# Offset convolutions two blocks ahead of the sampling, between an image's own steps

## The chip, the cores and the metric

The kernel runs on one core of a Trainium2 chip. The metric is the device time of one execution in microseconds, as the median of several runs. A profile was taken of one further execution.

## The reference

Four images of 256 channels and 64 by 64 pixels pass through two layers. This document is about the first, a deformable convolution with 3 by 3 taps:

```
x = groupnorm(x)                                    # 32 groups
om = conv3x3(x, w_off) + b_off                      # 27 channels
y, x positions = grid + tap + om[:18]               # per pixel and tap
mask = sigmoid(om[18:])
sampled = bilinear(x, positions) * mask             # four corners
out = einsum(sampled, w_conv)                       # 9 taps x 256 channels -> 256
```

Its sum with the input goes to the second layer: attention whose logits run over the images, and a mixture of eight experts of which each token takes two. Everything is float32.

## The kernel before

**Stages.** First comes the deformable convolution, image by image, then two passes of attention with routing, then the experts' tiles, then the weighing and the storing of the result. The change lies in the first stage alone.

**A sampling step.** A tile is 128 pixels, an image has 32 tiles (`NR`), each with 9 taps (`K2`), so an image has 288 steps (`STEPS`) and the whole stage 1152. For each image a table lies in memory (`tables[b]`), with two pixels, one above the other, in each row, so that one gathered run of 4 KB for each partition holds all four corners. A step n does the following:

- `gather` (L626, POOL): an indirect DMA from the table by the indices `params[b][0]` into one of ten buffers (`NGB`), two gathers every second step, ten steps ahead. The first of a pair waits for the last corner of step n + 1.
- `corner0` (L643, ScalarE) and `corner` (L651, VectorE, three a step) weigh the four corners with `params[b][1]` and add them into s.
- `turned` (L665, TensorE) transposes s, `to_sbuf` (L671, ScalarE) copies it out of PSUM, and `product` (L690, TensorE) multiplies it with the tap's weights into the tile's accumulator.
- `done` (L699 and L701) copies a finished tile out; after four tiles SP stores them.

On VectorE, ScalarE, TensorE and POOL the order of this loop is the order of the program (`manual_schedule`); SP's order is left to the planner.

**What an image needs first.** `pieces(b)` lists the preparation as pairs of a step and a function. `stats` (bn_stats, L332) at steps 32 to 47 and the group means after them give the scale and shift of the group norm; n is then 56. After that come eight blocks of 512 pixels (`NBLK`, `BLK`). `block(q, at)` can do two things:

- The table (`table`): `norm` (L393 or L395) normalises the block's rows into xs, `turn` and `leave` (L402, L415) transpose them, and four DMAs (L421) write them to the table.
- The offsets (`offsets`): TensorE multiplies ten rows of xs with the offset weights (`rows_of`, L433, 12 matmul instructions), ScalarE copies the result shifted for each of three taps (`shifted`, L445), TensorE adds these (`summed`, L454), and `kept` (L463) copies the 27 values of each pixel to SBUF.

`positions` (L492) then turns the offsets into indices and corner weights: 16 or 17 small operations on VectorE and one Sigmoid on ScalarE (L503).

**When.** Image 0's tables are made ahead of the first step, and so are the offsets of its first two blocks (`EARLY`). Its other six blocks' offsets lie between its own steps, at `(q - 2) * 36 + 12`, each followed by `positions` for that block's four tiles. Images 1 to 3 are prepared wholly during the image before: one block with table and offsets every 22 steps (`PERIOD`) from step 56, the offsets kept in a buffer for the whole image (`om`), and one call of `positions` for all 32 tiles at steps 235 to 251. So image 0's steps carry eight whole blocks of image 1 and six offset blocks of its own; those of images 1 and 2 carry eight whole blocks; those of image 3 carry none.

**Buffers.** The two images' raw data (`axs`), xs, the small tiles of `positions` (`atmp`) and the parameters are SBUF pools that stand one after another. The next stage's tiles reuse the same memory.

Of the kernel before, what the change touches and what calls it, by code (L numbers as in the profile page):

```python
# [9 lines left out]
F32 = mybir.dt.float32  # L10
# [7 lines left out]
P = 128  # L18
B, C, H, W = 4, 256, 64, 64
HW = H * W  # L20
NCH = C // P
K2 = 9
NR = HW // P
NOFF = 3 * K2
# [12 lines left out]
NT = BLK // P  # L37
# [3 lines left out]
STEPS = NR * K2  # L41
NGB = 10
AHEAD = NGB + 1
LOAD_AHEAD = 6
FIRST = 32
EARLY = 2
PERIOD = 22
NBLK = HW // BLK
GROUP = 8
# [29 lines left out]
def conv_attn_moe_kernel(  # L79
# [22 lines left out]
    nc = tc.nc  # L102
# [44 lines left out]
    def routed(rows, to, rw, ps_turned, ps_out, pool, name):  # L147


        pr, wTs = [], {}  # L150

        def turned(n):
            tp = ps_turned.tile([P, C], F32, name=f"{name}_tp{n}", tag="tp")
            for ch in range(NCH):
                T.transpose(tp[:, ch * P : (ch + 1) * P], rows[n][:, ch * P : (ch + 1) * P], ident)
            wTs[n] = pool.tile([P, C], F32, name=f"{name}_wT{n}", tag="sT")
            (V.tensor_copy if n % 2 else S.copy)(wTs[n], tp)

        def product(n):
            if not n:  # L160
                pr.append(ps_out.tile([P, len(rows), NX], F32, name=f"{name}_pr", tag="om"))
            for ch in range(NCH):
                T.matmul(
                    pr[0][:, n, :], wTs[n][:, ch * P : (ch + 1) * P], rw[:, ch, :],
                    start=(ch == 0), stop=(ch == NCH - 1),
                )

        for n in range(len(rows) + 1):
            if n < len(rows):
                turned(n)  # L170
            if n:
                product(n - 1)
            yield
        V.tensor_copy(to, pr[0].rearrange("p (ch k) n -> p ch k n", ch=NCH))
        yield
# [49 lines left out]
    with ExitStack() as actx:  # L225
        aw = actx.enter_context(tc.tile_pool(name="a_w", bufs=1))
        ag = actx.enter_context(tc.tile_pool(name="a_gather", bufs=1))
        asm = actx.enter_context(tc.tile_pool(name="a_sm", bufs=5))
# [4 lines left out]
        apad = actx.enter_context(tc.tile_pool(name="a_pad", bufs=2))  # L233
        atmp = actx.enter_context(tc.tile_pool(name="a_tmp", bufs=1))
        axs = [
            actx.enter_context(tc.tile_pool(name=f"a_x{i}", bufs=1)) for i in range(2)
        ]
        ps_tp = actx.enter_context(tc.tile_pool(name="ps_tp", bufs=4, space=PSUM))
        ps_om = actx.enter_context(tc.tile_pool(name="ps_om", bufs=2, space=PSUM))
# [77 lines left out]
        def pieces(b):  # L317
# [46 lines left out]

            xrv = xr.rearrange("p ch (h w) -> p ch h w", w=W)
            tv = tables[b].rearrange("(y x) (two c) -> y x two c", x=TW, two=2)
            om = atmp.tile([P, NR, NOFF], F32, name=f"om{b}", tag="om") if b else None

            def block(q, at, table=True, offsets=True, alone=False):

# [86 lines left out]
                        )  # L457

                def kept():
                    of[q] = om[:, rows_in(q), :] if b else atmp.tile(  # L460
                        [P, NT, NOFF], F32, name=f"om{b}_{q}", tag="om_", bufs=2
                    )
                    V.tensor_copy(of[q], t["pt"])  # L463

                out_.append((at, lambda: norm(0)))
# [21 lines left out]
            def rows_in(q):  # L487
                return slice(q * NT, (q + 1) * NT)
# [3 lines left out]
            def positions(rows, given, at, each):  # L492
                name = f"{b}_{rows.start}"
                nr = rows.stop - rows.start
                shape = [P, 2, nr, K2]
                t = {}

                def tmp(key, tag, dtype=F32, shape=shape):
                    t[key] = atmp.tile(shape, dtype, name=f"{key}{name}", tag=tag)
                    return t[key]  # L500

                def masked():
                    S.activation(  # L503
                        tmp("mask", "mask", shape=[P, nr, K2]), given()[:, :, 2 * K2 :],
                        AF.Sigmoid,
                    )

                def placed():
                    V.tensor_tensor(
                        tmp("pos", "pos"),  # L510
                        given()[:, :, : 2 * K2].rearrange("p r (k two) -> p two r k", two=2),
                        grid[:, :, rows], ALU.add,
                    )

                def indexed():
                    p0 = t["p0"]
                    V.tensor_scalar(
                        p0[:, 0], p0[:, 0], float(TW), float(TW + 1), ALU.mult, ALU.add
                    )
# [12 lines left out]

                def add(a, c):
                    V.tensor_tensor(a, a, c, ALU.add)

                def clamp():
                    V.tensor_scalar(t["pos"], t["pos"], -1.0, float(H), ALU.max, ALU.min)

                def compare():
                    V.tensor_tensor(tmp("over", "over"), t["p0"], t["pos"], ALU.is_gt)  # L540

                def rest():
                    V.tensor_tensor(tmp("lo", "over"), t["pos"], t["p0"], ALU.subtract)

                def other():
                    V.tensor_scalar(tmp("hi", "pos"), t["lo"], -1.0, 1.0, ALU.mult, ALU.add)

                done_ = []
                for i, fn in enumerate((
                    placed,  # L550
                    lambda: add(t["pos"], taps[:, :, rows]),
                    clamp,
                    lambda: V.tensor_copy(tmp("pi", "ki32", I32), t["pos"]),
                    lambda: V.tensor_copy(tmp("p0", "p0"), t["pi"]),
                    compare,
                    lambda: V.tensor_tensor(t["p0"], t["p0"], t["over"], ALU.subtract),
                    rest,
                    other,
                    indexed,
                    lambda: both("hi"),  # L560
                    lambda: both("lo"),
                    *(lambda c=c: weighted(c) for c in range(4)),
                )):
                    done_.append((at + i // each, fn))
                done_.append((at + 1, masked))
                return done_

            def place_for():
                params[b] = (
                    ap_.tile([P, NR, K2], I32, name=f"idx{b}", tag="idx"),  # L570
                    ap_.tile([P, 4, NR, K2], F32, name=f"wts{b}", tag="wts"),
                )

            if b:
                for q in range(NBLK):
                    block(q, n + q * PERIOD)
                n += (NBLK - 1) * PERIOD + 25
                later.append((n - 1, place_for))
                later.extend(positions(slice(0, NR), lambda: om, n, 1))
                assert n + 16 <= STEPS - AHEAD, n  # L580
                return later

            place_for()
            for q in range(NBLK):
                first.extend(block(q, n + 10 * q, offsets=False, alone=True))
            n += 10 * NBLK + 8
            for q in range(EARLY):
                at = n + 20 * q  # L590
                first.extend(block(q, at, table=False, alone=True))
                first.extend(positions(rows_in(q), lambda q=q: of[q], at + 25, 4))
            router = routed(
                [wconv_sb[:, ch, k, :] for ch in range(NCH) for k in range(K2)],
                wconv_sb[:, :, :, C:], rwc_sb, ps_tp, ps_om, asm, "wconv",
            )
            for m in range(NCH * K2 + 2):
                first.append((n + 10 + 1.5 * m, lambda: next(router)))
            for q in range(EARLY, NBLK):
                at = (q - 2) * NT * K2 + 12  # L600
                block(q, at, table=False)
                later.extend(positions(rows_in(q), lambda q=q: of[q], at + 25, 2))
                assert at + 33 <= q * NT * K2 - AHEAD, q
            order = {nc.vector.engine, nc.scalar.engine, nc.tensor.engine}
            with tc.manual_schedule(engines=order):
                emit(first)
            return later

        def emit(todo):
            for _, fn in sorted(todo, key=lambda p: p[0]):  # L610
                fn()
# [1181 lines left out]
```

## Time and profile before

| | us |
|---|---|
| median of 3 runs | 3588.42 (3581.35 to 3590.16) |
| the profiled execution | 3621.63 |
| its span, first to last instruction | 3619.9 |
| first sampling step of image 0, 1, 2, 3 | 73.1, 599.0, 1103.0, 1604.1 |
| last sampling step | 2121.7 |

Over the span TensorE's matmuls are busy 84%, VectorE 69%, POOL 54% and ScalarE 51%. An engine's busy share is a mean over stages with different limits, so the sampling steps are read by themselves. L643 runs exactly once a step; its start times, read from that line's instructions in the trace, give the pace of any stretch of steps.

### The profile page before, as it was taken

How to read it: one execution, taken by the hardware profiler on the slowest of the kernel's cores; microseconds unless marked ns; L12 is line 12 of the kernel's file. 1: busy time of each engine (PE TensorE's matmuls, PEld its weight loads, DVE VectorE, ACT ScalarE, POOL GpSimd, SP SyncE). 2: the span in 40 equal slices, each digit the busy share in tenths (PEclk: the TensorE clock that was granted, in tenths of full speed). 3: DMA queues.
4: the chain of work that ended last, by engine and by line, in shares of the span. 5: the costliest groups of instructions: out<-in, count | busy, mean ns of one | idle time of the engine just before them, and what ended most of it. 6: DMA issues, size and time to landing. Idle time of an engine off the chain costs nothing.

```text
span 3619.9 us, 49496 instructions
## 1 busy us (share of the span) xinstructions
PE 3041.8 (84%) x13658; PEld 2230.4 (62%) x13658; DVE 2480.5 (69%) x6303; ACT 1832.4 (51%) x4281; POOL 1961.6 (54%) x1818
## 2 busy tenths in 40 slices
PE   5899997899987899977777889997676588899996
PEld 4667665667665676656566655543343367788884
DVE  5867686777776777866666758875445555455887
ACT  2556554456554565544444457744344254455663
POOL 2555565666576665677666643305445536655441
PEclk8999998999998999989888989998788789999996
DMA  9889889899989899988787878723234334444888
GB/s 301 306 304 336 316 326 351 278 353 366 348 313 350 307 346 341 352 297 310 280 312 285 320 205 141 139 74 121 99 105 154 111 97 132 154 138 153 289 280 285
DMA packets 349897, 911.66 MB, mean 252 GB/s; under 512 B 43540, under 2 KB 123035, under 8 KB 347576
## 3 DMA queue, kind: packets, MB, share of 16 engines
q0 software_dynamic: 208704, 689.10, 55.1%
q1 hardware_dynamic: 140920, 219.39, 19.0%
q8 instruction: 113, 1.85, 0.2%
q14 instruction: 160, 1.31, 0.1%
HBM read 741.87 MB, written 170.12 MB: 252 GB/s over the span
## 4 chain that ended last, share of the span: by engine, by line
PE 48%; issue 14%; POOL 11%; DMA 9%; DVE 8%; another core or an unknown queue 6%; ACT 3%; SPq 0%; POOLq 0%; DVEq 0%; ACTq 0%
PE acc L690 13%; POOL g L626 10%; DMA g<-table,idx 6%; PE ph L1577 6%; PE py L1595 5%; PE tps L665 3%; PE po L433 3%; PE po L1129 3%; DVE s L651 3%; PE p_wq_sb L796 3%; PE p_wk_sb L796 3%; PE pg L796 2%; PE pv L796 1%; DVE mix L1098 1%
## 5 line engine op out<-in xcount | busy, mean ns | idle before, releaser
L651 DVE SCALAR_TENSOR_TENSOR s<-g,wts,s 128x256 f32<-128x256 f32 x3456 | 1433.5, 479 | 542.3 <-ACT s L643 374.3
L626 POOL DMA_INDIRECT g<-table,idx x1152 | 1310.4, 1137 | 765.7 <-DVE s L651 465.2
L690 PE MATMUL acc<-wconv_sb,sT 128*128 128x265 f32 x4608 | 1338.9, 415 | 274.3 <-ACT sT L671 165.7
L690 PEld LDWEIGHTS acc<-wconv_sb,sT 128*128 128x128 f32 x4608 | 832.4, 201 | 423.5 <-ACT sT L671 196.2
L671 ACT COPY sT<-tps 128x256 f32<-128x256 f32 x1152 | 425.4, 369 | 781.0 <-PE tps L665 489.9
L643 ACT ACTIVATE s<-g,wts 128x256 f32<-128x256 f32 x1152 | 588.9, 511 | 210.2 <-DMA g<-table,idx 180.9
L665 PE MATMUL tps<-ident,s 128*128 128x128 f32 x2304 | 461.7, 283 | 39.8 <-DVE s L651 37.8
L665 PEld LDWEIGHTS tps<-ident,s 128*128 128x128 f32 x2304 | 327.7, 148 | 270.1 <-issue 162.4
L1606 POOL DMA_INDIRECT ys_rows<-y,to x284 | 282.9, 996 | 299.9 <-DVE y L1603 225.2
L1577 PE MATMUL ph<-xT,w 128*128 128x256 f32 x1136 | 282.8, 392 | 35.6 <-DVE second L1563 18.3
L1273 POOL DMA_INDIRECT xs_rows<-u,slots x256 | 250.0, 976 | 94.6 <-issue 88.8
L1595 PE MATMUL py<-w,hT 128*128 128x256 f32 x1136 | 270.7, 381 | 0.0
L1581 ACT ACTIVATE hT<-ph,w 128x256 f32<-128x256 f32 x284 | 132.7, 474 | 237.2 <-PE ph L1577 170.0
L1577 PEld LDWEIGHTS ph<-xT,w 128*128 128x128 f32 x1136 | 210.3, 196 | 66.6 <-ACT hT L1581 18.4
L1600 DVE TENSOR_TENSOR y<-py,w 128x512 f32<-128x512 f32 x142 | 98.2, 691 | 206.8 <-ACT w L1539 70.7
L1595 PEld LDWEIGHTS py<-w,hT 128*128 128x128 f32 x1136 | 218.3, 192 | 30.5
L1098 DVE SCALAR_TENSOR_TENSOR mix<-pv,att,mix 128x512 f32<-128x512 f32 x192 | 131.0, 742 | 142.6 <-remote 106.3
L1103 ACT ACTIVATE gate<-pg,bg_c 128x512 f32<-128x512 f32 x64 | 43.8, 688 | 277.1 <-DVE mix L1118 190.1
L919 DVE SCALAR_TENSOR_TENSOR junk<-q,k 128x512 f32<-128x512 f32 x256 | 162.1, 687 | 24.6 <-ACT k L900 24.4
L433 PE MATMUL po<-xs,woff_sb 128*96 128x512 f32 x288 | 152.4, 612 | 0.0
L796 PE MATMUL pg<-early_state,wg_sb 128*128 128x512 f32 x160 | 87.1, 680 | 76.9 <-DVE mix L1098 61.8
L1178 POOL TENSOR_TENSOR rstd<-l3var,nhalf 128x8 f32<-128x8 f32 x16 | 26.5, 1656 | 215.1 <-DVE l3var L1176 207.2
(264 smaller groups left out, 3432.1 us busy)
## 6 DMA issues: line engine op xcount, KB each, us to landing
xt<-xs_rows SPq DMA_DIRECT2D x142, 260.0 KB
table<-zt SPq DMA_DIRECT2D x96, 256.0 KB
yk<-ys_rows SPq DMA_DIRECT2D x80, 256.0 KB
g<-table,idx POOLq DMA_INDIRECT x1152
t<-o SPq DMA_DIRECT2D x32, 530.0 KB
t<-bo_sb POOLq DMA_DIRECT2D x32, 530.0 KB
dt<-t SPq DMA_DIRECT2D x64, 265.0 KB
xraw<-in_x SPq DMA_DIRECT2D x16, 1024.0 KB
```

The costliest lines, as they stand in the source:

```text
L433: T.matmul(t["po"], woff_sb[:, ch, ki].rearrange("p kj o -> p (kj o)"), t["xs"][:, ch, ki : ki + RB], start=(n == 0), stop=(n == NCH * 3 - 1),
L626: g = G.indirect_dma_start(out=gs[n % NGB], out_offset=None, in_=tables[b], in_offset=bass.IndirectOffsetOnAxis(ap=params[b][0][:, r, k : ...
L643: first = S.activation(ss[n], gs[n % NGB][:, :C], AF.Copy, scale=params[b][1][:, 0, r, k : k + 1])
L651: last_corner[n] = V.scalar_tensor_tensor(ss[n], gs[n % NGB][:, c * C : (c + 1) * C], params[b][1][:, c, r, k : k + 1], ss[n], ALU.mult, A ...
L665: T.transpose(tps[n][:, ch * P : (ch + 1) * P], s[:, ch * P : (ch + 1) * P], ident)
L671: S.copy(sTs[n], tps.pop(n))
L690: T.matmul(accs[n // K2][:, :CR], sT[:, ch * P : (ch + 1) * P], wconv_sb[:, ch, k, :], start=False, stop=(k == K2 - 1 and ch == NCH - 1),)
L796: T.matmul(ps, w[:, ci, ch * P : (ch + 1) * P], src[:, ci, :], start=(ci == 0), stop=(ci == NCH - 1),)
L1273: s = G.indirect_dma_start(out=rows_, out_offset=bass.IndirectOffsetOnAxis(ap=slots[:, k, n : n + 1], axis=0), in_=u[:, n % NT, :], in_off ...
L1577: T.matmul(ph, w1_sb[:, ch, f * P : (f + 1) * P], xT[:, ch, :], start=(ch == 0), stop=(ch == NCH - 1),)
L1595: T.matmul(py[:, i, :], hT[:, f, i * P : (i + 1) * P], w2_sb[:, f, :], start=(f == 0), stop=(f == NCH - 1),)
L1606: s = G.indirect_dma_start(out=ys_rows[g], out_offset=bass.IndirectOffsetOnAxis(ap=to[:, i : i + 1], axis=0), in_=y[:, i, :], in_offset=No ...
```

## The change

The change treats every image as image 0 is treated. During the image before, only its tables are made (blocks without offsets, every 22 steps), and the offsets of its first two blocks, at steps 212 and 232 (`EARLY_AT`), with their positions. The other six blocks' offsets, each with the positions of four tiles, lie between its own steps at `(q - 2) * 36 + 12`. A table block normalises its own eight rows; the offset block normalises its ten rows again, into a buffer of its own (`xs_`). The buffer `om` for a whole image and the positions over 32 tiles are gone, and the raw data of images 1 and 3 move to the other end of SBUF.

```diff
+EARLY_AT = 212
...
-            actx.enter_context(tc.tile_pool(name=f"a_x{i}", bufs=1)) for i in range(2)
+            actx.enter_context(tc.tile_pool(name=f"a_x{i}", bufs=1, side=("left", "right")[i]))
+            for i in range(2)
...
-            om = atmp.tile([P, NR, NOFF], F32, name=f"om{b}", tag="om") if b else None
...
-                    of[q] = om[:, rows_in(q), :] if b else atmp.tile(
-                        [P, NT, NOFF], F32, name=f"om{b}_{q}", tag="om_", bufs=2
-                    )
+                    of[q] = atmp.tile([P, NT, NOFF], F32, name=f"om{b}_{q}", tag="om", bufs=2)
...
-            if b:
+            if b == 0:
+                place_for()
                 for q in range(NBLK):
-                    block(q, n + q * PERIOD)
-                n += (NBLK - 1) * PERIOD + 25
+                    first.extend(block(q, n + 10 * q, offsets=False, alone=True))
...
+            else:
                 later.append((n - 1, place_for))
-                later.extend(positions(slice(0, NR), lambda: om, n, 1))
-                assert n + 16 <= STEPS - AHEAD, n
-                return later
...
+                for q in range(NBLK):
+                    block(q, n + q * PERIOD, offsets=False)
+                for q in range(EARLY):
+                    at = EARLY_AT + 20 * q
+                    block(q, at, table=False)
+                    later.extend(positions(rows_in(q), lambda q=q: of[q], at + 25, 2))
+                    assert at + 33 <= STEPS - AHEAD
             for q in range(EARLY, NBLK):
                 at = (q - 2) * NT * K2 + 12
+                assert at + 33 <= q * NT * K2 - AHEAD, q
+                at += STEPS if b else 0
                 block(q, at, table=False)
                 later.extend(positions(rows_in(q), lambda q=q: of[q], at + 25, 2))
-                assert at + 33 <= q * NT * K2 - AHEAD, q
```

More of the change, by code (lines that the diff above doesn't have):

```diff
@@ L572, in place_for @@
                 )
-            if b:
+            if b == 0:
+                place_for()
                 for q in range(NBLK):
-                    block(q, n + q * PERIOD)
-                n += (NBLK - 1) * PERIOD + 25
-                later.append((n - 1, place_for))
-                later.extend(positions(slice(0, NR), lambda: om, n, 1))
-                assert n + 16 <= STEPS - AHEAD, n
-                return later
-            place_for()
-            for q in range(NBLK):
-                first.extend(block(q, n + 10 * q, offsets=False, alone=True))
@@ L588, in pieces @@
[L588 to L598, printed above, removed]
+                    first.extend(block(q, n + 10 * q, offsets=False, alone=True))
@@ new lines, in pieces @@
+                n += 10 * NBLK + 8
+                for q in range(EARLY):
+                    at = n + 20 * q
+                    first.extend(block(q, at, table=False, alone=True))
+                    first.extend(positions(rows_in(q), lambda q=q: of[q], at + 25, 4))
+                router = routed(
+                    [wconv_sb[:, ch, k, :] for ch in range(NCH) for k in range(K2)],
+                    wconv_sb[:, :, :, C:], rwc_sb, ps_tp, ps_om, asm, "wconv",
+                )
+                for m in range(NCH * K2 + 2):
+                    first.append((n + 10 + 1.5 * m, lambda: next(router)))
+            else:
+                later.append((n - 1, place_for))
+                for q in range(NBLK):
+                    block(q, n + q * PERIOD, offsets=False)
+                for q in range(EARLY):
+                    at = EARLY_AT + 20 * q
+                    block(q, at, table=False)
+                    later.extend(positions(rows_in(q), lambda q=q: of[q], at + 25, 2))
+                    assert at + 33 <= STEPS - AHEAD
@@ L599, in pieces @@
             for q in range(EARLY, NBLK):
                 at = (q - 2) * NT * K2 + 12
+                assert at + 33 <= q * NT * K2 - AHEAD, q
+                at += STEPS if b else 0
                 block(q, at, table=False)
                 later.extend(positions(rows_in(q), lambda q=q: of[q], at + 25, 2))
-                assert at + 33 <= q * NT * K2 - AHEAD, q
-            order = {nc.vector.engine, nc.scalar.engine, nc.tensor.engine}
-            with tc.manual_schedule(engines=order):
-                emit(first)
+            if b == 0:
+                order = {nc.vector.engine, nc.scalar.engine, nc.tensor.engine}
+                with tc.manual_schedule(engines=order):
+                    emit(first)
```

## The prediction

> **What bounds the kernel now.** I read the page first, then the summary by stretches, then the waits of two stretches, then single lines. The page gives the span and the groups that fill the sampling steps.
>
> ```profile
> span 3619.9 us, 49496 instructions
> ...
> L651 DVE SCALAR_TENSOR_TENSOR s<-g,wts,s 128x256 f32<-128x256 f32 x3456 | 1433.5, 479 | 542.3 <-ACT s L643 374.3
> L626 POOL DMA_INDIRECT g<-table,idx x1152 | 1310.4, 1137 | 765.7 <-DVE s L651 465.2
> L690 PE MATMUL acc<-wconv_sb,sT 128*128 128x265 f32 x4608 | 1338.9, 415 | 274.3 <-ACT sT L671 165.7
> L671 ACT COPY sT<-tps 128x256 f32<-128x256 f32 x1152 | 425.4, 369 | 781.0 <-PE tps L665 489.9
> L643 ACT ACTIVATE s<-g,wts 128x256 f32<-128x256 f32 x1152 | 588.9, 511 | 210.2 <-DMA g<-table,idx 180.9
> ```
>
> 1152 sampling steps run from 73 us to 2122 us; only they, and what is put between them, are touched. L643 runs once a step, so the start of every 36th one gives the pace. Images 0 to 3 take 526, 504, 501 and 518 us. Image 3, which has nothing between its steps, is no faster than images 1 and 2, which prepare a whole image. The stretches show it (steps 72 to 252 of images 0, 1, 2, then all of image 3):
>
> ```profile
> core 0: us, PE busy (x) PEld busy (x) DVE busy (x) ACT busy (x) POOL busy (x), PEclk, DMA share, GB/s
> 207.30:528.10 320.80, 302.23 (x1494) 223.34 (x1493) 242.37 (x647) 195.02 (x474) 186.83 (x181) 0.98 0.92 328
> 731.40:1028.90 297.50, 278.09 (x1408) 210.16 (x1408) 230.15 (x559) 180.01 (x449) 186.20 (x179) 0.99 0.97 356
> 1233.00:1534.70 301.70, 280.77 (x1407) 211.75 (x1408) 229.21 (x557) 179.48 (x449) 185.60 (x179) 0.98 0.95 345
> 1604.10:2122.00 517.90, 403.04 (x1912) 319.03 (x1911) 355.13 (x863) 232.95 (x607) 350.33 (x288) 0.87 0.84 302
> ```
>
> In the filled stretches PE is busy 93 to 94% of the time at full clock: PE bounds them. In image 3 PE is busy 78% at 0.87, DMA 84%: nothing is full. What it waits for, beside image 1's filled stretch (us in total, times, longest):
>
> ```profile
> ACT sT L671 <- remote: 70.5, 18, 6.3
> ...
> ACT s L643 <- DMA g<-table,idx: 52.2, 44, 4.9
> ```
>
> (image 3, 1668 to 2061 us), and from 731 to 1029 us:
>
> ```profile
> ACT sT L671 <- remote: 14.6, 8, 4.1
> ```
>
> So light stretches lose time to two kinds of pause, each about every 20 steps: ScalarE stands still for 3 to 6 us ahead of a sT copy, and a gather holds POOL for up to 8.8 us instead of 0.95 (mean 1.23 us in image 3, 1.04 in image 1's filled stretch). Other engines run dry in each. In filled stretches POOL's pauses are gone and ScalarE's are short. **Light steps are pause-bound, filled ones PE-bound.**
>
> **What the Trainium skill says.** (1) "TensorE: Matmul & The Clock Gate", section on HAM oscillation: PE gaps longer than some 3.4 us bring the clock down. Agrees: 0.87 in image 3, 0.98 to 0.99 where filled. (2) "DMA: Bandwidth & Descriptors", section on SWDGE vs HWDGE vs iDMA: POOL writes descriptors into rings in SBUF, and VectorE's two-port modes lock POOL out of it. The trace fits: around 508 to 520 us, under the 576-wide position operations, gathers took 1.55 us for 0.95; whether the long ones have that cause no run shows. (3) "ScalarE: Activation LUTs", section on what ACT_TABLE_LOAD costs, has a load at 1.28 us plus a drain. The trace has 1283 ns, seven times, and none between 53 and 2386 us: more Sigmoids cost no loads.
>
> **The change, part by part.** Steps are counted within an image.
>
> *Where blocks go.* Offset blocks stay 32, tables the same. Image 0's steps lose 6 blocks, image 3's gain 6; images 1 and 2 give and get 6 each, now one per 36 steps instead of one per 22.
>
> *Price of a block in filled steps.* Image 0's steps 72 to 228 hold tables and offsets of image 1 (one block per 22 steps) and its own offsets (one per 36): 1803 ns a step. The same steps of images 1 and 2, without own offsets: 1658 and 1690, mean 1674. One block per 36 steps costs 129 ns a step, **4.6 us a block**.
>
> *Image 0, steps 72 to 228.* New load: tables per 22, one offset block per 36. Linear: 1803 - 4600/22 = 1594. Floor: lighter steps bring pauses back, so I take 1665, between 1594 and 1740. (1803 - 1665) x 156 = **-21.5 us** (-33 to -10).
>
> *Images 1 and 2, same steps.* The same load from 1674: 9 ns x 312 = **-3 us** (-25 to +20).
>
> *Image 3.* Six blocks on steps 12 to 228, now 1825 ns. One stretch shows offsets alone between the steps: image 0, steps 12 to 48, 97.9 to 159.2 us, 1703 ns; the same steps of images 1, 2 and 3 take 1797, 1789 and 1835. It is short, and image 0's first, so I take 1745: 80 x 216 = **-17 us** (-38 at 1650, +28 if six blocks cost 4.6 us each with all pauses kept).
>
> *Images 1 and 2, steps 12 to 48.* They get a block as well: 1793 to about 1735, x 72 = **-4 us** (-7 to +9). At steps 36 to 72 bn_stats reigns: 1935 ns with offsets (image 0), 1939 and 1931 without, so nothing there.
>
> *Positions.* Instead of 16 VectorE operations of 0.45 to 0.75 us (some 8.6 to 9 us an image), eight sets of 3.4 us (17 instructions, as in image 0): +19 us of VectorE an image, 57 in all, 2 a step. Cover: VectorE is busy 77% of a filled step, 69% in image 3. The long ones go, and perhaps the 9.2 us gather that follows them at step 251 in images 0, 1 and 2; pauses tend to come back elsewhere, so **-4 us** (-20 to +12).
>
> *Second normalisation.* 16 more ScalarE operations an image: 0.926 us for 640 elements and 0.869 for 576 make some 0.81 us for the tables' 512, an estimate; 13 us an image, 39 in all. Cover: ScalarE is busy 60% of filled steps, and fewer oc copies per step make room: 0 (to +13).
>
> *At nothing.* The norm waits for the one xs_ buffer, whose last matmul lies at least two steps back; behind it on ScalarE stand L643 and L671, for which VectorE and PE wait. A group's indices are ready 17 steps (29 us) ahead of its first gather, first rows 33 steps; gathers read idx while VectorE writes other rows, as image 0 has it already. POOL's memsets stay as many. No DMA is added, table stores and image loads keep their steps, so SP's queue keeps its order but for the five weight loads of the next stage (1539 us now): om's going and the new side move memory, and they may wait for image 3's last positions, about 2010 us, with L701's stores behind them: 0 (to +8). PE's total work is unchanged.
>
> **Sum:** -21.5 - 3 - 17 - 4 - 4 = -49.5, say -50 us. The profiled execution took 3621.63 us (span 3619.9), 33 above the median of the runs, 3588.42; the pauses may be a little longer in it. I put the difference on the median: **3538 us**.
>
> **Rivals.** *Pauses nearly vanish:* image 3 falls to 1650, the mixed stretches to 1594: -38 - 33 - 25 - 4 = -100, **3488**. For it: no long gather between 360 and 500 us, nor between 740 and 1000; against: ScalarE's pauses stay there.
>
> *A wash:* image 3 keeps its pace, pauses and blocks trading places, second norms and small position operations eat image 0's gain: -21.5 + 20 = about 0, **3588**. For it: image 0's steps 12 to 48 are one sample, and with bn_stats offsets changed nothing.
>
> *Slower: image 3's blocks lie in series.* ScalarE, PE and VectorE wait for each other in order every step; if pauses come on a clock of their own, six blocks add 6 x 4.6 = +28; a third of the norms, +13; a fifth of the small positions, +11; image 0 gives back 24: +28, **3616**. It decides as soon as image 3 comes out above some 1900 ns a step over steps 12 to 228. Against it: images 1 and 2 are faster than 3 under more work.
>
> *It doesn't do what it says:* block times and waits follow from the steps, so the spread will be there; only its worth is in doubt.
>
> **How the numbers follow.** Main case (-80 to -20) 0.58, pauses vanish 0.08, wash 0.11, slower 0.23. About 0.3%, 11 us, is what a measurement of this kernel can tell from no change. Faster 0.66, same 0.11, slower 0.23. Range 3500 to 3612: it leaves out most of the vanishing case and the upper half of the slower one, under 0.2 together; the main case alone is 3508 to 3568.
>
> **What would show it.** Right: image 0 near 503 us, images 1 and 2 near 500, image 3 near 500; over its steps 12 to 228 PEclk above 0.93, L626's mean under 1.15 us, the remote wait of L671 below half of 70 us; mask 128x36 in every image, no lump of VectorE work at steps 235 to 251. Wrong: image 3 above 530 us with pauses as before, or the mixed stretches of images 1 and 2 above 1720 ns with long gathers in them; or a later start of the stage after sampling.

## The result and the profile after

The changed kernel takes **3647.07 us** (median of 4, 3616.01 to 3653.76) where the kernel before takes 3589.29 us in the same comparison: a ratio of **1.0124**, 95% interval 1.0084 to 1.0165. By the ratio it is slower by some 45 us (the two medians lie 58 us apart); the forecast was 50 us faster. The profiled execution took 3650.27 us, 28.6 more than that of before.

The page's span and the groups that fill a sampling step, of the changed kernel (lines stand three lower than before: L629 is the gather, L654 the corners, L646 corner 0, L674 the sT copy, L693 the product):

```profile
span 3648.6 us, 49907 instructions
...
L654 DVE SCALAR_TENSOR_TENSOR s<-g,wts,s 128x256 f32<-128x256 f32 x3456 | 1439.8, 479 | 529.3 <-ACT s L646 383.2
L629 POOL DMA_INDIRECT g<-table,idx x1152 | 1322.1, 1148 | 780.5 <-DVE s L654 477.9
L693 PE MATMUL acc<-wconv_sb,sT 128*128 128x265 f32 x4608 | 1337.5, 415 | 283.4 <-ACT sT L674 172.5
L674 ACT COPY sT<-tps 128x256 f32<-128x256 f32 x1152 | 424.7, 369 | 806.5 <-PE tps L668 478.2
L646 ACT ACTIVATE s<-g,wts 128x256 f32<-128x256 f32 x1152 | 588.2, 511 | 184.7 <-DMA g<-table,idx 136.7
```

Nothing here tells the two kernels apart: each row stands within 1% of its old duration. The summary by stretches (again steps 72 to 252 of images 0, 1, 2, then image 3) does:

```profile
core 0: us, PE busy (x) PEld busy (x) DVE busy (x) ACT busy (x) POOL busy (x), PEclk, DMA share, GB/s
204.60:533.40 328.80, 285.28 (x1376) 212.21 (x1376) 238.60 (x649) 181.95 (x459) 201.95 (x182) 0.94 0.90 321
733.40:1055.80 322.40, 284.10 (x1372) 217.20 (x1371) 237.53 (x648) 180.45 (x456) 202.77 (x182) 0.93 0.91 325
1246.10:1572.20 326.10, 284.98 (x1368) 215.38 (x1369) 237.43 (x647) 180.15 (x455) 202.94 (x182) 0.93 0.91 322
1636.30:2148.30 512.00, 428.24 (x2036) 328.60 (x2035) 369.50 (x970) 252.24 (x644) 343.96 (x287) 0.92 0.85 304
```

The filled stretches of images 1 and 2 were the kernel's best (298 and 302 us). Now all three look alike: PE is busy 87 or 88% of the time, no longer 93 to 94%, its clock fell from 0.98 or 0.99 to 0.93, and POOL is busy for 15 to 17 us longer **with the same number of gathers**. Only image 3 gained. Taken apart by steps, from the starts of L646:

| stretch | forecast, us | measured, us |
|---|---|---|
| image 0, steps 72 to 228 | -21.5 | +3 (1803 to 1821 ns a step) |
| images 1 and 2, the same steps | -3 | +38 (1658 and 1690 to 1782 and 1811) |
| image 3, steps 12 to 228 | -17 | -13 (1825 to 1763) |
| images 1 and 2, steps 12 to 48 | -4 | -4 |
| all other sampling steps (the forecast is its term for the positions, to which it gave no place) | -4 | +3 |
| after the last step | 0 | +2 |

**A held gather, read closely.** The timeline of POOL in image 3, after the positions of an offset block (start, us taken, operation, idle time before it):

```profile
1847.98 0.95 POOL L629 DMA_INDIRECT g<-table,idx  x1 [0.33 <-issue]
1849.23 5.85 POOL L629 DMA_INDIRECT g<-table,idx  x1 [0.30 <-issue]
1855.39 0.95 POOL L629 DMA_INDIRECT g<-table,idx  x1 [0.30 <-DVE s L654]
```

And the timeline of VectorE in the same microseconds:

```profile
1846.84 1.26 DVE L654 SCALAR_TENSOR_TENSOR s<-g,wts,s 128x256 f32<-128x256 f32 x3
1848.03 0.18 DVE L525 TENSOR_TENSOR wts<-hi,lo 128x36 f32<-128x36 f32 x1
1848.13 0.18 DVE L525 TENSOR_TENSOR wts<-lo 128x36 f32<-128x36 f32 x1
1848.24 6.02 DVE L654 SCALAR_TENSOR_TENSOR s<-g,wts,s 128x256 f32<-128x256 f32 x15
1854.55 1.29 DVE L654 SCALAR_TENSOR_TENSOR s<-g,wts,s 128x256 f32<-128x256 f32 x3 [0.29 <-ACT s L646]
```

A set is the small operations of one call of `positions` for four tiles. While it runs, two operations a step, VectorE has hardly a gap and falls behind. When the last one is through, at 1848.2, it works off five waiting steps: 15 corners without a gap between them (a gap-free run), to 1854.26. The gather issued at 1849.23 lasts until 1855.08, **0.82 us after that run ended**. Across the sampling steps 38 gathers took over 1.5 us; 29 of them end 0.81 to 0.83 us after such a run, and 6 more 0.36 to 0.48 us before the end of one. The 5.85 us ones stand at gathers 91, 127, 163, 199, then 379, 415, 487, and on to 1063 (counted from 0 over the four images), at most one per 36 steps, where a set ends.

What it costs shows in the stretches around it:

```profile
1840.00:1850.00 10.00, 9.17 (x48) 6.78 (x48) 9.15 (x31) 6.34 (x18) 5.80 (x6) 1.00 0.98 373
1850.00:1855.00 5.00, 4.96 (x28) 3.99 (x28) 4.71 (x13) 3.67 (x10) 5.00 (x1) 1.00 0.46 166
1855.00:1862.00 7.00, 6.18 (x28) 4.40 (x29) 5.38 (x14) 3.53 (x10) 5.17 (x7) 1.00 0.83 286
1862.00:1870.00 8.00, 4.62 (x25) 3.33 (x24) 4.30 (x11) 2.52 (x7) 6.17 (x7) 1.00 0.98 357
```

During the hold PE is at its fullest, 4.96 of 5 us, on data that had landed; the DMA share falls from 0.98 to 0.46. The bill comes later: from 1862 to 1870 PE works 4.62 of 8 us. In steps 72 to 228 of all images, the 12 steps that follow a hold of over 4.5 us take 2167 ns each, all others 1642: 180 such steps x 525 ns = 94 us. Before it was 86 steps at 2123 against 1689 ns, 37 us. An estimate that puts this whole difference down to the holds gives them some 57 us more, and the lighter steps some 29 us less, which makes the +28 us of these stretches together. The place of these steps is not what makes them slow: the same 180 steps take 1543 ns each, and the others 1664, in the run after_psum of the second round, where no gather is held.

**What the Trainium skill has on it.** The page "SBUF — State Buffer", section "Who interferes with whom", says that a VectorE instruction with two SBUF inputs contends with a GpSimd instruction that reads SBUF, and calls the shared port an exclusive lock, held for the whole instruction. A corner has two SBUF tensors as inputs (g and s). The same section infers that writing descriptors does not need the side of the port that such an instruction takes, so the page does not settle this case. The trace fits a lock but differs on its length: the gather lasts for a run of instructions, 5 us, not for one of 0.48. Nor is every gather held that meets such a run: of 70 issued with over 3 us of gap-free corners ahead, 28 were held; in before_again, on the second kind of chip below, it was 8 of 328. What picks them out no run here shows.

### The profile page after: what moved, and what is told of

The parts are those of the page before. It is cut to its first block, busy times and chain, and to the rows that moved or that the text cites. A ratio compares the mean times of both kernels' runs of the same rounds, so it can differ in the third digit from the quotient of the medians.

```text
span 3648.6 us, 49907 instructions
## 1 busy us (share of the span) xinstructions
PE 3055.9 (84%) x13658; PEld 2235.2 (61%) x13658; DVE 2511.4 (69%) x6660; ACT 1860.1 (51%) x4350; POOL 1973.3 (54%) x1818
## 4 chain that ended last, share of the span: by engine, by line
PE 49%; issue 14%; POOL 9%; DVE 9%; DMA 7%; another core or an unknown queue 7%; ACT 4%; SPq 0%; POOLq 0%; ACTq 0%; DVEq 0%
PE acc L693 14%; POOL g L629 9%; PE ph L1580 6%; DMA g<-table,idx 5%; PE py L1598 5%; PE tps L668 4%; DVE s L654 3%; PE po L1132 3%; PE po L434 3%; PE p_wq_sb L799 3%; PE p_wk_sb L799 3%; PE pg L799 3%; PE pv L799 2%; PE tpx L1559 1%
## 5 line engine op out<-in xcount | busy, mean ns | idle before, releaser
L654 DVE SCALAR_TENSOR_TENSOR s<-g,wts,s 128x256 f32<-128x256 f32 x3456 | 1439.8, 479 | 529.3 <-ACT s L646 383.2
L629 POOL DMA_INDIRECT g<-table,idx x1152 | 1322.1, 1148 | 780.5 <-DVE s L654 477.9
L693 PE MATMUL acc<-wconv_sb,sT 128*128 128x265 f32 x4608 | 1337.5, 415 | 283.4 <-ACT sT L674 172.5
L693 PEld LDWEIGHTS acc<-wconv_sb,sT 128*128 128x128 f32 x4608 | 828.9, 201 | 436.6 <-ACT sT L674 213.7
L674 ACT COPY sT<-tps 128x256 f32<-128x256 f32 x1152 | 424.7, 369 | 806.5 <-PE tps L668 478.2
L646 ACT ACTIVATE s<-g,wts 128x256 f32<-128x256 f32 x1152 | 588.2, 511 | 184.7 <-DMA g<-table,idx 136.7
L1181 POOL TENSOR_TENSOR rstd<-l3var,nhalf 128x8 f32<-128x8 f32 x16 | 26.5, 1656 | 211.8 <-DVE l3var L1179 203.9
L1132 PE MATMUL po<-wo_sb,mix 128*128 128x265 f32 x512 | 124.0, 401 | 12.4 <-DVE s L1150 12.4
```

Source lines behind the costliest of these rows:

```text
L629: g = G.indirect_dma_start(out=gs[n % NGB], out_offset=None, in_=tables[b], in_offset=bass.IndirectOffsetOnAxis(ap=params[b][0][:, r, k : ...
L646: first = S.activation(ss[n], gs[n % NGB][:, :C], AF.Copy, scale=params[b][1][:, 0, r, k : k + 1])
L654: last_corner[n] = V.scalar_tensor_tensor(ss[n], gs[n % NGB][:, c * C : (c + 1) * C], params[b][1][:, c, r, k : k + 1], ss[n], ALU.mult, A ...
L674: S.copy(sTs[n], tps.pop(n))
L693: T.matmul(accs[n // K2][:, :CR], sT[:, ch * P : (ch + 1) * P], wconv_sb[:, ch, k, :], start=False, stop=(k == K2 - 1 and ch == NCH - 1),)
L1132: T.matmul(po[:, n, :CR], o[:, ch, i * P : (i + 1) * P], wo_sb[:, ch, :], start=(ch == 0), stop=(ch == NCH - 1),)
```

## The experiments

Theory H (holds): the sets drive VectorE into gap-free runs, and these hold gathers. Rivals: N, the second normalisation is on the path; S, image 3's blocks simply add up in series; W, the sets cost as work, wherever they lie. The expectations call H theory A, and N with S theory B; that is not the A and B of the chips. The runs come from chips of two kinds, on which the same kernel before takes about 3540 to 3600 us (A, the kind of the result above) or 3137 to 3142 (B). On B the waits of the sT copy for "remote" (a release that the trace ascribes to another core or an unknown queue) are absent. Ratios compare with the kernel before on the same chip only.

**First round, chip B: is it the positions?**

before_again is the kernel before. after_nopos and before_nopos leave the positions of images 1 to 3 out, so that these images sample with image 0's indices and weights:

```diff
+                if b:
+                    return []
                 name = f"{b}_{rows.start}"
...
-                params[b] = (
+                params[b] = params[0] if b else (
```

after_each1 spreads a set over 17 steps, one operation in each:

```diff
-                    later.extend(positions(rows_in(q), lambda q=q: of[q], at + 25, 2))
+                    later.extend(positions(rows_in(q), lambda q=q: of[q], at + 25, 1))
```

Expected of before_again: 

> The kernel before, unchanged, profiled once more. The first profiled execution took 3621.63 us where the median of its runs is 3589 us. If the pauses of POOL and ScalarE fall differently from one execution to the next, this profile lies near 3590 us and shows fewer held gathers than the 49 over 1.5 us of the first (148 us of excess over 0.95 us); if the profile itself costs the 33 us, it lies near 3620 us again with about 49 held gathers. The ratio to the kernel before is 1.000 either way.

Expected of after_nopos: 

> The change, with the positions of images 1 to 3 left out (they use image 0's indices and weights). Theory A (the small position operations put VectorE behind, it then runs without a gap, and a gather is held on POOL till the run ends): the held gathers at every 36th step (5.85 us each, some 15 in images 1 to 3) vanish, images 1 and 2 fall from 518 us to about 495, and the whole comes to 3560 to 3600 us. Theory B (the second normalisation on ScalarE and blocks without cover, VectorE innocent): the gain is the VectorE time alone at most, 3620 to 3640 us, and held gathers stay at their steps.

Expected of before_nopos: 

> The kernel before, with the positions of images 1 to 3 left out (image 0's are used). It is the yardstick for the other kernel without positions. Three lumps of 9 us of VectorE and their 9.2 us held gathers go: theory A 3570 to 3585 us. The difference to the change without positions is what remains of the change: theory A about 0 (-30 to +10 us), theory B +40 us or more.

Expected of after_each1: 

> The change with the positions spread, one VectorE operation a step over 16 steps in place of two over 8. Theory A: VectorE falls behind less, so the run without gaps after each set is shorter or absent: 3590 to 3630 us, held gathers shorter than 5.85 us or gone. Theory B: nothing changes, 3640 to 3655 us.

| kernel | median, us | ratio (95%) | images 0 to 3, us |
|---|---|---|---|
| before_again | 3136.53 | 0.9997 (0.9986 to 1.0008) | 483.3, 449.6, 442.7, 389.6 |
| after_nopos | 3122.17 | 0.9944 (0.9927 to 0.996) | 453.4, 444.0, 446.7, 410.0 |
| before_nopos | 3115.84 | 0.9929 (0.9913 to 0.9946) | 476.2, 438.7, 439.2, 388.4 |
| after_each1 | 3111.21 | 0.9918 (0.9901 to 0.9934) | 448.7, 446.2, 438.3, 407.4 |

The same small operations one a step instead of two, none left out, cost no more than no positions at all. That is against W in this plain form. But image 3 stayed 18 us above its old time on this kind of chip, so S has a part there. Nor did the holds simply go in after_nopos, as expected: no gather of images 1 to 3 takes 5.85 us at the old places, but 29 still take over 1.5 us, among them those behind image 0's own sets (127, 163 and 199) and shorter ones 36 apart in image 3 (911, 947 and 983, of 2.5 to 2.9 us).

**Second round, chip A: the holds, the second norm, and the operand.**

after_again is the changed kernel. after_nonorm leaves out the second normalisation of images 1 to 3 (their offset blocks read image 0's last normalised rows). after_shift2 starts each set two steps later (`at + 27`). after_psum keeps s in PSUM until its last corner, so that a corner has one SBUF tensor as input; the transposes give up two of their four PSUM banks for it:

```diff
-        ps_tp = actx.enter_context(tc.tile_pool(name="ps_tp", bufs=4, space=PSUM))
+        ps_tp = actx.enter_context(tc.tile_pool(name="ps_tp", bufs=2, space=PSUM))
+        ps_s = actx.enter_context(tc.tile_pool(name="ps_s", bufs=2, space=PSUM))
...
-                    ss[n], gs[n % NGB][:, c * C : (c + 1) * C],
-                    params[b][1][:, c, r, k : k + 1], ss[n], ALU.mult, ALU.add,
+                    ss[n] if c == 3 else sp[n], gs[n % NGB][:, c * C : (c + 1) * C],
+                    params[b][1][:, c, r, k : k + 1], sp[n], ALU.mult, ALU.add,
```

Expected of after_again: 

> The change, unchanged, beside the kernel before on one chip. The kernel before took 3589 us where it was predicted and 3137 us in the first round of experiments; there ScalarE's pauses ahead of the sT copies are gone and image 3's light steps take 1.35 us, not 1.80. Theory A (small position sets drive VectorE into runs without gaps, which hold gathers): slower than its spread form, at 0.993 to 1.005 of before where before takes 3137 us, 1.008 to 1.016 where it takes 3589 us, held gathers of 5.85 us at every 36th step in both. Theory B (no cover in image 3 for blocks and second norms): image 3 alone is longer, by 6 x 4.6 = 28 us, where its light steps take 1.35 us, ratio above 1.005.

Expected of after_nonorm: 

> The change, with the second normalisation of images 1 to 3 left out: their offset blocks read the last rows that image 0 normalised. ScalarE loses 48 operations of 0.92 us, 44 us. Theory B: faster than the change by 10 to 30 us. Theory A: within 8 us of the change, held gathers as before.

Expected of after_shift2: 

> The change with each later set of positions two steps on. Held gathers have numbers that leave 3 when divided by 4, and the one at every 36th step is issued just as VectorE ends its set. If only such gathers can be held (theory A's finer form), the next one comes two steps on, when the set ends, so the phase is the same only if it follows the set and not the number: the held gather stays 91 + 36 k with a hold shorter than 5.85 us, or moves to 95 + 36 k with one of 2 to 4 us, and the whole is 5 to 15 us faster than the change. If the number plays no part, it moves to 93 + 36 k with 5.85 us, and the time is the same within 5 us.

Expected of after_psum: 

> The change with the weighted sum s held in PSUM until the last corner (two of the four transpose banks go to it), so that VectorE reads one operand of SBUF instead of two in each of the three corner operations. If it is VectorE's second SBUF operand that keeps POOL out (theory A's cause), held gathers in the runs without gaps go, but for those under the position sets: 20 to 50 us faster than the change. If VectorE's operands play no part, the held gathers stay and the time is equal or up to 20 us longer for the fewer transpose banks.

| kernel | median, us | ratio (95%) | images 0 to 3, us |
|---|---|---|---|
| after_again | 3644.94 | 1.0137 (1.01 to 1.0174) | 518.7, 522.9, 520.6, 505.2 |
| after_nonorm | 3658.2 | 1.0172 (1.012 to 1.0223) | 521.9, 531.9, 527.9, 520.1 |
| after_shift2 | 3588.87 | 0.9958 (0.9936 to 0.998) | 508.5, 502.4, 510.3, 485.8 |
| after_psum | 3486.08 | 0.9677 (0.964 to 0.9715) | 482.8, 481.9, 483.5, 462.4 |

N finds no support on this kind of chip: without the second norm the kernel is no faster. (Its holds grew as well: what its gathers of over 1.5 us took above 0.95 us sums to 193 us, against 133 in after_again, so the norm's own price stays hidden.) The most telling is after_shift2: the same instructions two steps later are worth 56 us, where at most 15 had been expected. Its gathers, as the trace sums them for the line (shortest, median, longest in ns):

```profile
L629 POOL DMA_INDIRECT g<-table,idx x1142: 932/948/9417, 81.0 to 2072.4; - x191
```

and those of after_psum:

```profile
L631 POOL DMA_INDIRECT g<-table,idx x1142: 932/944/1011, 89.7 to 1985.7; - x191
```

In after_shift2 the periodic holds moved with the sets, to gathers 93, 129, 165, and shrank to 2.3 to 3.5 us; a finer guess, that only every fourth gather is held, fell with that. In after_psum not one gather is held: the longest took 1.011 us in place of 9.4, though VectorE works more, 75% of the span for 69. Its page (L660 is the corners, L699 the product):

```profile
span 3484.9 us, 49739 instructions
...
L631 POOL DMA_INDIRECT g<-table,idx x1152 | 1086.7, 943 | 856.6 <-DVE s L660 483.3
...
L699 PE MATMUL acc<-wconv_sb,sT 128*128 128x265 f32 x4608 | 1259.9, 396 | 42.3 <-ACT sT L680 32.1
```

The edit does more than take one SBUF input away, though. Two corners in three now write to PSUM, and the corners no longer run without a gap: where one follows another within 0.65 us, the time from start to start is 396 ns (median) in the changed kernel, less than the 479 that one takes, so they overlap; in after_psum it is 514 ns, as in these three of its timeline:

```profile
1004.90 0.48 DVE L660 SCALAR_TENSOR_TENSOR sp<-g,wts,sp 128x256 f32<-128x256 f32 x1
1005.42 0.48 DVE L660 SCALAR_TENSOR_TENSOR s<-g,wts,sp 128x256 f32<-128x256 f32 x1
1005.94 0.49 DVE L660 SCALAR_TENSOR_TENSOR sp<-g,wts,sp 128x256 f32<-128x256 f32 x1
```

The corners keep VectorE busy for 1551 us in place of 1440, and no gap-free run of them is longer than 1.8 us, against 92 of over 3 us in the changed kernel. Whether the missing SBUF input or the gaps free the gathers, no run separates.

PE's wait ahead of a product fell from 283.4 to 42.3 us. With the holds went ScalarE's pauses. The waits of the changed kernel and of after_psum over the sampling (us in total, times, longest):

```profile
ACT sT L674 <- remote: 223.7, 64, 7.9
```

```profile
ACT sT L680 <- remote: 14.9, 8, 4.8
```

So either these pauses follow from VectorE's access to SBUF too, or s in PSUM removes them in another way. The runs do not decide it, and the gain of after_psum is not that of the holds alone.

**Third round, chip A: the change without holds, and one part of it alone.** before_psum keeps s in PSUM in the kernel before. before_split only cuts the positions over 32 tiles into eight sets of four, two operations a step after each block (with tags of their own for each image), and leaves all blocks where they were:

```diff
                     block(q, n + q * PERIOD)
+                    later.extend(positions(
+                        rows_in(q), lambda q=q: om[:, rows_in(q), :], n + q * PERIOD + 25, 2
+                    ))
-                n += (NBLK - 1) * PERIOD + 25
-                later.extend(positions(slice(0, NR), lambda: om, n, 1))
```

Expected of before_psum: 

> The kernel before, with s in PSUM until the last corner. Holds make up 148 us of POOL's time in before's profile, as much as in the change's. Theory A: the held gathers go here as well, and it lies at 0.965 to 0.985 of before where that takes 3590 us. Its image 0 keeps its overload, about 1.75 us a step at steps 72 to 212, which the change without holds does not have (1.63 us): then the change is worth 10 to 35 us once no gather is held. If it lies at or under the change with s in PSUM, moving the blocks is worth nothing even then.

Expected of after_psum_again: 

> The change with s in PSUM, once more, beside the kernel before with s in PSUM on the same chip: 0.967 of before where before takes 3590 us; where before takes 3137 us there is little to hold (61 us of excess), and I expect 0.975 to 0.99.

Expected of before_split: 

> The kernel before, with one part of the change alone: the positions of images 1 to 3 in eight sets of four tiles, each after its block, in the image before, in place of one call for 32 tiles; blocks and normalisation stay. Theory A's plain form (every small set is followed by a hold): 24 holds of 2 to 5 us in place of three of 9 us, 3610 to 3650 us where before takes 3590. If holds need VectorE to fall behind in steps that PE does not bound, the filled stretches of images 1 and 2 stay free of them and the time is that of before within 10 us.

Expected of after_each1_again: 

> The change with the positions spread over 16 steps, on this chip: it lay at 0.9918 of before where that takes 3137 us. Two steps' shift made the holds 3.47 us for 5.85 and gave 56 us at 3590 us; one operation a step leaves VectorE less behind. Theory A: 0.98 to 1.00 of before.

| kernel | median, us | ratio (95%) | images 0 to 3, us |
|---|---|---|---|
| before_psum | 3443.26 | 0.9723 (0.9679 to 0.9768) | 500.1, 467.8, 468.0, 441.7 |
| after_psum_again | 3433.8 | 0.9703 (0.9659 to 0.9747) | 473.6, 479.7, 475.8, 446.7 |
| before_split | 3552.1 | 1.0031 (1.001 to 1.0052) | 514.4, 498.5, 492.4, 506.2 |
| after_each1_again | 3511.14 | 0.9922 (0.9884 to 0.9961) | 506.8, 485.5, 481.3, 485.8 |

With no gather held in either, the change is worth -26.5 us in image 0 and +12, +8 and +5 in images 1 to 3: about 10 us in all by the medians, of which the sampling steps make 2. The order change without the holds is nearly a wash, slightly good. before_split shows that going from one lump to sets of two a step is no gain by itself, but no great loss either: some 11 us by the ratio, where the plain form of H had expected 20 to 60, with 44 gathers over 1.5 us where the profile of the kernel before has 49. So, next to the lumps that they replace, the sets cost much on this kind of chip only together with the changed kernel's order of blocks. And the changed kernel with one operation a step takes less time than both kernels here too; its gathers in the page:

```profile
L629 POOL DMA_INDIRECT g<-table,idx x1152 | 1233.3, 1071 | 753.3 <-DVE s L654 458.6
```

The mean is 1071 ns instead of 1148; 23 gathers still took over 1.5 us.

**Fourth round, chip B: the terms without holds.** The PSUM form of the changed kernel (psum_ref), and with it each edit of above: no second norm, no positions (both for images 1 to 3, as above), one operation a step.

Expected of psum_ref: 

> The change with s in PSUM, without held gathers, as the yardstick of this round: 0.967 to 0.971 of before where before takes 3540 to 3600 us.

Expected of psum_nonorm: 

> The same, with the second normalisation of images 1 to 3 left out (their offset blocks read image 0's last normalised rows). If ScalarE's 44 us lie in part on the path once nothing holds the gathers: 5 to 20 us faster than the yardstick. If they are covered, as the prediction had it: within 4 us.

Expected of psum_nopos: 

> The same as the yardstick, with the positions of images 1 to 3 left out (image 0's indices and weights are used). VectorE loses 24 sets of some 3.4 us, 82 us. If VectorE's time is covered once POOL is not kept out: within 5 us of the yardstick. If VectorE itself is near the bound: 15 to 40 us faster.

Expected of psum_each1: 

> The same as the yardstick, with the positions spread over 16 steps. Without holds the spreading has nothing to shorten: within 4 us of the yardstick. If the sets delay the sampling by themselves as lumps, it gains 5 to 15 us, and is the fastest correct version.

| kernel | median, us | ratio (95%) |
|---|---|---|
| psum_ref | 3223.17 | 1.0266 (1.025 to 1.0282) |
| psum_nonorm | 3207.89 | 1.0212 (1.0198 to 1.0227) |
| psum_nopos | 3183.53 | 1.014 (1.0124 to 1.0155) |
| psum_each1 | 3186.67 | 1.0147 (1.0132 to 1.0163) |

The first expectation missed its sign: on B, s in PSUM makes the kernel slower, by 61 us against the changed kernel of the next round. Part of it may be VectorE's: the corners keep it busy for 1550 us, against 1444 in after_third, since they overlap less; part may be the two transpose banks it took. No run separates the two. In this form the second norm costs 15 us and the sets 40, and spreading them gives 36 of these back **with no gather held**. So part of W is true as well, on this kind of chip and in this form: two small operations in one step cost time without any hold, where one a step costs next to nothing (psum_each1 lies 3 us above psum_nopos).

**Fifth round, chip B: the changed kernel, with and without the sets.** after_third is the changed kernel, after_nopos_again as after_nopos.

Expected of after_third: 

> The change, unchanged, as the yardstick for the next kernel on the same chip. Where before takes 3540 to 3600 us: 1.010 to 1.016 of it. Where before takes 3140 us: the change with its positions spread lay at 0.992, the one without them at 0.994, and sets of two a step cost 36 us more than spread ones with s in PSUM; so 0.998 to 1.008.

Expected of after_nopos_again: 

> The change with the positions of images 1 to 3 left out, beside the change on the same chip. Theory A where before takes 3540 to 3600 us: the held gathers at every 36th step go, 40 to 80 us faster than the change, 0.99 to 1.00 of before. Where before takes 3140 us it lay at 0.9944, and the change beside it tells what the sets cost there: 20 to 40 us.

| kernel | median, us | ratio (95%) | images 0 to 3, us |
|---|---|---|---|
| after_third | 3161.73 | 1.0072 (1.0052 to 1.0092) | 455.9, 456.6, 449.8, 426.1 |
| after_nopos_again | 3125.49 | 0.9962 (0.9945 to 0.9978) | 446.7, 447.3, 441.8, 408.7 |

The sets cost 36 us here too, so the change is slower on both kinds of chip, but by another split: against before_again, image 0 gains 27 us, images 1 and 2 lose 7 each, and image 3 loses 36.5. Its steps 12 to 228 went from 1350 to 1481 ns: +28 us, the number that the slower rival had worked out for six blocks in series. That is luck: without the sets the same steps lose 19 us (1439 ns), and with them spread 15 (1420 ns).

The 5.85 us gathers stand at the same places (127, 199, 415, 487, 703, then 919 to 1063), but here they cost little. By the count used above, the 12 steps that follow a hold of over 4.5 us take 1570 ns each and all others 1495: 132 steps x 75 ns = 10 us, where the profile of the change on A gave 94. So H explains little of the 36 us on B; there W fits better, since with s in PSUM spreading the sets gave the same 36 without any hold.

## Why the prediction was wrong, step by step

**Positions: the step that failed.** The prediction put small operations two a step at -4 us (-20 to +12), with VectorE's 77% busy as their cover. On A, the same operations one a step take the changed kernel from 1.0124 to 0.9922 of the kernel before, some 70 us; starting them two steps later gives back 56. On B, taking them out gives back 36. The lumps of the kernel before had a price as well, 21 us on B (before_again against before_nopos), so the term as the prediction meant it, sets in place of lumps, is 36 - 21 = +15 us there. With the operations spread, the change is 28 us faster than the kernel before on A: the terms for the blocks had the right sign.

The busy share was read rightly and used wrongly: 23% idle is room for the work, but the work came before the waiting corners. On A a VectorE that is behind catches up without a gap, gathers are held in these runs, and the steps after a hold are slow. On B the holds are there and cost little; by the runs with s in PSUM the pairs cost there as work in the order of the step. "What is late next" was asked of the engines that wait for VectorE, not of POOL. The profile before had a sign: two of image 0's own sets, which end at 227.4 and 357.1 us, are followed at once by gathers of 4.83 and 3.47 us (91 and 163), in a stretch of which the prediction says that POOL's pauses are gone. It had even named long gathers as the sign of being wrong, with the mixed stretches above 1720 ns: it came, 1782 and 1811.

**Image 0, -21.5.** Right in size where holds are absent or cost little: -20 in these steps with s in PSUM, -25 on B. In the profile after it was +3. Image 0's own sets, which the kernel before has too, are there followed by four holds of 5.85 us (91, 127, 163 and 199) in place of the two of 4.83 and 3.47; that these took the gain back is likely, and not shown by a run of its own.

**Images 1 and 2, -3 (-25 to +20).** Measured +38, outside its bounds, and the largest miss. With s in PSUM on A it is +14, and on B 0, both inside. The price of 4.6 us for a block was taken from image 0's steps, which held the same sets; but the linear sum of tables and offsets left no place for an interaction. In its filled stretches the kernel before had hardly a long gather; the change put one after nearly every set.

**Image 3, -17 (-38 to +28).** -13 on A: right. On B, where image 3 ran at 1350 ns a step and had no ScalarE pauses to lose, +28 for those steps, and still +15 with the sets spread. The argument that light steps are pause-bound can hold on A alone.

**Steps 12 to 48, -4,** and **the work after the last step, 0**: measured -4 and +2, right on A. On B steps 12 to 48 lose 13 us.

**Second norm, 0 (to +13).** No gain from leaving it out on A, where longer holds hide its price; 15 us with s in PSUM on B, just above the bound. For A it stays open.

**Other signs.** PEclk in image 3's steps 12 to 228 came to 0.93 and the gathers' mean to 1.148 us, at the limits that were named. The remote wait fell only from 70.5 to 58.7 us, not below half. The lump of VectorE work and its 9.2 us gather at step 251 did go, but gathers of 9.4 us came back elsewhere (275, 851 and 1099).

**The slower rival** got the sign, 3616, but on A not its mechanism: image 3 gained. Its term for the positions, a fifth of them or +11, was too small: a fifth of the 56 us that two steps of delay were worth, a third of the 36 us on B.

**What stays open.** How ScalarE's remote pauses arise; whether it is the second SBUF input or the missing gaps that hold gathers, and which of those that meet a gap-free run; how the 56 us between the two placements on A divide between holds and the order of the step; why holds cost much on A and little on B; how much of the loss of s in PSUM on B is VectorE's.

## What to carry to other kernels

An engine's idle share covers added work only if that work does not stand ahead of something already waiting, and if catching up holds nobody else: look at the longest gather, not the mean, and at what the other engines do when it ends. Put small operations one to a step rather than in pairs: here that takes 1.0124 to 0.9922 on A and 1.0072 to 0.9918 on B, the one correct version tried here on both that is faster than both kernels. A larger gain that was seen on one kind of chip only, as s in PSUM (0.9677 on A, 1.0266 on B), is to be tried on others before it is kept.

## What the runs showed of the hardware

- A gather's 0.95 us on POOL can grow to 9.4 us. In the changed kernel 29 of the 38 that took over 1.5 us end 0.81 to 0.83 us after a gap-free run of VectorE operations with two SBUF inputs. With s in PSUM, which also opens gaps between these operations (after_psum), the longest of 1142 is 1.011 us.
- The same held gathers go with 525 ns more for each of the next 12 steps on one kind of chip (after), and with 75 ns on the other (after_third).
- A corner from PSUM to PSUM takes 486 ns instead of 479, but corners that follow each other within 0.65 us start 514 ns apart (median, after_psum) instead of 396 (after).
- One kernel takes 3540 to 3600 us on some chips and 3140 on others. In the profiles of the kernel before, 202.9 us of remote waits on the sT copy stand against none, and the stages after the sampling take 1498 us against 1295.
